# Attention in front of quantised convolutions: the products with exponentials take the transposed image, and the output projection moves behind the normalisation

## The chip, the cores and the metric

The kernel runs on one core of a Trainium2 chip. The metric is the device time of one execution in microseconds (us), lower is better. The engines are named as in the profile: PE is TensorE's matmul and PEld its weight load, DVE is VectorE, ACT is ScalarE, POOL is GpSimd, SP is SyncE.

## The reference

The input is a batch of 16 images of 128 channels and 32 x 32 pixels. Layer 0 is attention with 4 heads over the 1024 pixels of an image, and a residual; layer 1 is two 3 x 3 convolutions with 4-bit activations and weights, each followed by a batch norm over the whole batch.

```python
qkv = einsum('bchw,oc->bohw', x, w_qkv) + b_qkv          # 4 heads, 3 x 128 channels each
scores = einsum('bnc,bcm->bnm', q, k) * c ** -0.5         # 1024 x 1024 per head
attn = softmax(scores, axis=-1)
out = einsum('bnm,bmc->bnc', attn, v)                     # heads side by side: 512 channels
x = einsum('bchw,oc->bohw', out, w_out) + b_out + x       # layer 0

out = conv3x3(act_quant(x), weight_quant(w1))
out = batchnorm(out, gamma1, beta1)
out = conv3x3(act_quant(out), weight_quant(w2))
x = batchnorm(out, gamma2, beta2) + x                     # layer 1
```

`act_quant` clips to 0..1 and rounds to 15 levels, `weight_quant` rounds to 7 levels on each side.

## The kernel before

All of it stands in `fast_path`. A channel is a partition, and a pixel is a column. The weights of a head are folded at the start: query and key weights into one 128 x 128 matrix `at_sb`, value and output weights into another, `bt_sb` (`fold_a`, `fold_b`). So a head needs `u = at x` (`project_u`), scores as products of `x` with `u`, exponentials, and products of the exponentials with `vo`, which is the image already behind the value and output weights (`project_v`). The product of exponentials and `vo` is then the head's share of the output, not yet divided by the sums.

The attention phase is one loop of steps. A head `g` has `NK = 4` steps, and 63 of the 64 heads are done in this way; the last one is cut into 16 smaller units at the end. A step `k` of a head takes two blocks of 128 keys (`k` and `k + 4`) and all 1024 queries:

- `scores(g, k)`: four score tiles of 128 x 512, three PSUM banks in turn (`ps_s`), and an exponential on ScalarE for each. VectorE then makes the sums and differences T3, T1 and T2, T4 of the four blocks and adds T4 and T3 to the running sums `es`.
- `attend(g, k - 1)` for the step before: seven products of 64 x 512 in place of eight. They are a fast scheme for 2 x 2 blocks: blocks of the exponentials and their sums on one side, blocks of the values and their sums `S1` to `S4` on the other. They add up in four banks, `a0` to `a3`, over the four steps of the head.
- every f32 product is issued as two halves of 64 output rows (`halves`), which run side by side on the array.

What else a head or an image needs is hung on a step and on one of its halves with `at(step, half, fn)`: half 0 is run between `scores` and `attend`, half 1 behind `attend`. `end = (g + 1) * NK` is the first step after a head. On it hang `sum_up` (the head's sums), `evacuate` (four copies from PSUM to `ev`), `combine` in three parts (small copies of 64 partitions on ScalarE, L605 to L615, additions on VectorE, L608 to L618), and `normalise` (`end + 2`, half 1). In `normalise` the head's output is multiplied by the inverse sums and added to `accs[b]`; the last head of an image adds the bias and the image too, and stores it to `x1d`:

```python
if h == 0:
    nc.vector.tensor_tensor(accs[b], av, rb, ALU.mult)                      # L673
    return
nc.vector.tensor_tensor(av, av, rb, ALU.mult)                               # L675
nc.vector.tensor_tensor(accs[b], accs[b], av, ALU.add)                      # L676
if h == NH - 1 or g == LAST - 1:
    nc.vector.scalar_tensor_tensor(accs[b], accs[b], bo2_sb, xt[b], ALU.add, ALU.add)   # L679
```

Behind the last head of an image come `quantize`, `transform_rows`, four `rows_product` (the first convolution in a row-filtered form, bf16, PSUM tiles `psw`), `rows_output` and `first_statistics`. `project_v` of the next image makes eight tiles `psv`, spread over six steps; ScalarE copies each to `vo` (L530), VectorE makes the sums of blocks (L532, L533). `psu`, `psv` and `psw` all use the one bank of the pool `ps_m`, each freed by a copy on ScalarE.

TensorE's order is as written: each product is chained behind the one before (`issue_after`). On the other engines the framework orders the instructions by its own estimate of when their operands are there, so `quantize` and the like can stand between the operations of a step, and loads can stand earlier than where they are written.

At the end of attention the units of the last head alternate `score_unit` and `attend_unit`; `normalise_group` finishes three groups of columns, each with its row sums from a small product `psr` in the bank of `ps_m`; `first_conv` follows. The second part of the kernel does the batch norms and the second convolution and writes the output.

Of the kernel before, what the change touches and what calls it, by code (L numbers as in the profile page):

```python
# [191 lines left out]
def fast_path(  # L192
    nc, tc, x, wqk, wvo, bo, bnp, x1d, y1d, out, bo_sb, bnp_sb, quad, wq, sc, flag, conv_weights,
# [179 lines left out]
    with ExitStack() as ph:  # L373
# [4 lines left out]
        vp = pool("vo", 5)  # L378
        ep = pool("e", 2)
        esp = pool("es", 1)  # L380
        avp = pool("av", 1)
# [13 lines left out]
        xt, us, vos, es, sides, avs, psa, accs, evs = {}, {}, {}, {}, {}, {}, {}, {}, {}  # L395
# [20 lines left out]
        def load(b, queue=nc.sync):  # L416
            xt[b] = xp.tile([P, N], F32, tag="x", name=f"x{b}")
            queue.dma_start(out=xt[b], in_=x[b])

# [10 lines left out]
        nc.sync.dma_start(out=wvo_sb[0 : P // 2], in_=wvo[0 : P // 2])  # L430
        nc.scalar.dma_start(out=wvo_sb[P // 2 :], in_=wvo[P // 2 :])

        def load_rest(behind):

            with tc.issue_after(behind):
                nc.scalar.dma_start(out=wqk_sb[:, 1:], in_=wqk[:, 1:])
                nc.scalar.dma_start(out=bo_sb, in_=bo)
                nc.scalar.dma_start(out=bnp_sb, in_=bnp)
# [11 lines left out]

        bt_sb = once.tile([P, 2, NH + 1, P], F32, name="bt_sb")
        bo2_sb = once.tile([P, 1], F32, name="bo2_sb")

        def place_of(b, h):

            return h if b == B - 1 else (h + 1) % NH
# [15 lines left out]
        def fold_b():  # L474
            ps = ps_m.tile([P, NH, P], F32, tag="mm", name="ps_b")
            for h in range(NH):
                product(ps[:, h, :], wvo_sb[:, h, 0:P], wvo_sb[:, h, P : 2 * P])
            nc.scalar.copy(bt_sb[:, 1, 1:], ps)
            nc.vector.tensor_copy(bt_sb[:, 1, 0], ps[:, NH - 1])
            nc.scalar.copy(bt_sb[:, 0, :, TOP], bt_sb[:, 1, :, TOP])  # L480
            nc.vector.tensor_tensor(
                bt_sb[:, 0, 0:NH, BOTTOM], bt_sb[:, 1, 0:NH, BOTTOM], bt_sb[:, 1, 0:NH, TOP], ALU.subtract
            )
            nc.vector.tensor_copy(bt_sb[:, 0, NH, BOTTOM], bt_sb[:, 1, NH, BOTTOM])
# [30 lines left out]

        A11, A12, S3, A22, S2, S1, S4 = range(7)
# [3 lines left out]
        def project_v(b, k, c, ps=None):  # L520

            if ps is None:
                ps = ps_m.tile([P, HALF], F32, tag="mm", name=f"psv_{b}_{k}_{c}")
            first = int(b == B - 1)
            weights = bt_sb[:, c, first : first + NH].rearrange("p h o -> p (h o)")
            halves(ps, lambda t: xt[b][:, ts((k + NK * c) * 2 + t, PH)], weights)
            if c == 0:
                vos[b, k] = vp.tile([P, 7, NH, PH], F32, tag="vo", name=f"vo_{b}_{k}")
            v = vos[b, k]
            nc.scalar.copy(v[:, c : c + 3 : 2], ps.rearrange("p (h a o) -> p a h o", a=2, o=PH))  # L530
            if c == 1:
                nc.vector.tensor_tensor(v[:, S2], v[:, S3], v[:, A22], ALU.subtract)  # L532
                nc.vector.tensor_tensor(  # L533
                    v[:, S1 : S4 + 1],
                    v[:, A11 : A12 + 1],
                    v[:, S2 : S2 + 1].to_broadcast([P, 2, NH, PH]),
                    ALU.add,
                )

# [3 lines left out]
        def scores(g, k, between=None):  # L543
# [4 lines left out]
            for i, (c, m) in enumerate(((0, 1), (1, 1), (0, 0), (1, 0))):  # L548
                ps = ps_s.tile([P, HALF], F32, tag="s", name=f"pss_{g}_{k}_{i}")
                score(ps, b, g, k + NK * c, ts(m, HALF))  # L550
                exps[:] = [nc.scalar.activation(e[:, 2 * c + 1 - m], ps, AF.Exp).ins]  # L551
                if between and i in between:
                    between[i]()
# [13 lines left out]
        def attend(g, k):  # L567
            b, h = heads[g]
            e, v = es.pop((g, k)), vos[b, k][:, :, place_of(b, h)]
# [6 lines left out]
            seven = [(0, 0, A11, B11), (1, 1, A22, T4), (1, 0, A12, B21), (2, 1, S2, T2)]  # L576
            seven += [(2, 0, S4, B22), (3, 1, S1, T1)]
            if k % 2:
                seven = [seven[i] for i in (1, 0, 3, 2, 5, 4)] + [(0, 1, S3, T3)]
            else:  # L580
                seven += [(3, 0, S3, T3)]
            for n, (bank, t, value, exponential) in enumerate(seven):
                product(
                    psa[g][bank][LANES[t]],
                    v[:, value],
# [81 lines left out]
        def normalise(g):  # L667
            b, h = heads[g]
            rb = inverse_sums(g, sides.pop(g), slice(0, N))
            av = avs.pop(g)  # L670
            if h == 0:
                accs[b] = accp.tile([P, N], F32, tag="acc", name=f"acc_{b}")
                nc.vector.tensor_tensor(accs[b], av, rb, ALU.mult)  # L673
                return
            nc.vector.tensor_tensor(av, av, rb, ALU.mult)  # L675
            nc.vector.tensor_tensor(accs[b], accs[b], av, ALU.add)  # L676
            if h == NH - 1 or g == LAST - 1:

                nc.vector.scalar_tensor_tensor(accs[b], accs[b], bo2_sb, xt[b], ALU.add, ALU.add)  # L679
            if h == NH - 1:  # L680
# [26 lines left out]
        def attend_unit(u):  # L707
# [18 lines left out]
            for m, key in enumerate(keys):  # L726
                c, k = divmod(key, NK)
                v = vos[b, k][:, :, place_of(b, h)]
# [3 lines left out]
                        lambda t: v[:, (A11, S3)[t] + c],  # L732
# [129 lines left out]
        at(NK, 0, fold_bo)  # L862
# [7 lines left out]
        for g in range(LAST):  # L870
# [12 lines left out]
            if h == NH - 1:  # L883
                at(end + 3, 0, lambda b: quantize(b, accs[b], A_LEVELS, 0.0), b)
                at(end + 3, 1, sums_range, b)
                at(end + 4, 0, transform_rows, b)
                for i, k in enumerate((1, 2, 0, 3)):
                    at(end + 6 + (i + 1) // 2, (i + 1) % 2, rows_product, b, k)
                at(end + 8, 1, rows_output, b)
                at(end + 9, 0, first_statistics, b)  # L890
                if b + 2 < B:
                    at(end + 5, 0, load, b + 2, nc.scalar)
            elif h == NH - 2 and b + 1 < B:

                when = ((4, 0), (4, 1), (6, 1), (7, 0), (7, 1), (8, 0), (8, 1), (9, 1))
                for i, (step, half) in enumerate(when):
                    at(g * NK + step, half, project_v, b + 1, *divmod(i, 2))
# [4 lines left out]
        for step in range(n_steps):  # L902
            g, k = divmod(step, NK)
            between = {}
            if step == 1:
                banks = [ps_a.tile([P, HALF], F32, tag=f"a{2 + c}", name=f"psv_0_{c}") for c in range(2)]
                between = {0: lambda: project_v(0, 0, 0, banks[0]), 1: lambda: project_v(0, 0, 1, banks[1])}
            scores(g, k, between)
            if step == 0:
                fold_b()  # L910
            elif step < NK:
                project_v(0, step, 0)
# [3 lines left out]
            if 0 < step < NK:  # L916
                ps = ps_s.tile([P, HALF], F32, tag="s", name=f"psv_0_{step}_1")
                project_v(0, step, 1, ps)
# [3 lines left out]
        for u in range(n_units):  # L922
# [5 lines left out]
            if u > 3:  # L928
                for _ in range(2 if u in (8, 9) else 1):
                    attend_unit(next_)  # L930
                    next_ += 1
                    if next_ == FIRST_UNIT[1]:
                        at(n_steps + 2, 1, normalise_group, 0)
# [259 lines left out]
def attention_then_quantized_convs(  # L1193
    ctx: ExitStack,
    tc: tile.TileContext,
    x: bass.AP,
    wqk: bass.AP,
# [45 lines left out]
    def conv_weights(n, wp, behind):  # L1243
# [22 lines left out]
        nc, tc, x, wqk, wvo, bo, bnp, x1d, y1d, out, bo_sb, bnp_sb, quad, wq, sc, flag, conv_weights,  # L1266
# [83 lines left out]
```

## Time and profile before

| | |
|---|---|
| median of two runs | 2023.55 us (2023.24 to 2023.87) |
| profiled execution | 2024.57 us |
| its span | 2022.7 us |
| granted clock in it | 0.993 |
| busy: PE, PEld | 1987.6, 730.3 us |
| busy: DVE, ACT, POOL | 1722.2, 1198.5, 19.7 us |
| moved by DMA | 43.74 MB |

A line of the groups gives line and engine, the operation, what is written and read, how many there were, then busy time and the mean of one in ns, then the idle time of the engine before them and what ended it. A product of TensorE leaves two records if it is f32. A line of the timeline begins with start and length in us.

### The profile page before, as it was taken

What the parts mean: (1) busy time and instruction counts of PE and PEld (TensorE: products, weight loads), DVE (VectorE), ACT (ScalarE), POOL (GpSimd) and SP (SyncE); (2) the same over time, 40 slices, a digit from 0 to 9 for tenths busy, and PEclk for the clock granted to TensorE, in tenths of its full rate; (3) what the DMA queues carried; (4) which work ended last, traced back from release to release, by engine and by line L of the source; (5) the groups of instructions that cost most, each with busy time, mean ns of one, the idle gap of its engine ahead of it and who ended that gap; (6) DMA issues with size and microseconds to landing.
All of it is one profiled execution on the core that took longest, in us unless ns stands there. A gap on an engine that the chain in (4) does not pass through costs nothing. (4 is left out here: it accounts for less than half of the span.)

```text
span 2022.7 us, 24701 instructions
## 1 busy us (share of the span) xinstructions
PE 1987.6 (98%) x9497; PEld 730.3 (36%) x9497; DVE 1722.2 (85%) x2642; ACT 1198.5 (59%) x2007; POOL 19.7 (1%) x29
## 2 busy tenths in 40 slices
PE   9999999999999999999999999999999999999994
PEld 3543333333333333333333333433333333333441
DVE  5889888888888888888888888888888888878888
ACT  4565665665566566566556556656656655655575
POOL 0000000000000000000000000000000000000020
PEclk9999999999999999999999999999999999999997
DMA  1000000000000000000000000000000000000064
GB/s 42 24 1 22 1 22 1 22 0 1 22 1 22 1 9 14 0 22 1 21 1 1 22 1 21 11 22 11 1 22 11 22 11 21 11 1 11 11 239 168
DMA packets 12846, 43.74 MB, mean 22 GB/s; under 512 B 1456, under 2 KB 1840, under 8 KB 12720
## 3 DMA queue, kind: packets, MB, share of 16 engines
q1 hardware_dynamic: 9520, 32.05, 4.2%
q10 hardware_dynamic: 3200, 10.03, 1.5%
q8 instruction: 76, 1.25, 0.3%
q14 instruction: 50, 0.41, 0.1%
HBM read 22.16 MB, written 19.92 MB: 21 GB/s over the span
## 5 line engine op out<-in xcount | busy, mean ns | idle before, releaser
L403 PE MATMUL pss<-u,x 128*64 128x512 f32 (+1 forms) x4128 | 1031.9, 589 | 1.6 <-ACT u L509 1.6
L403 PE MATMUL psa<-e,vo 128*64 128x512 f32 (+1 forms) x3624 | 922.4, 588 | 0.0
L551 ACT ACTIVATE e<-pss 128x512 f32<-128x512 f32 x1008 | 595.4, 596 | 380.7 <-PE pss L403 331.9
L403 PEld LDWEIGHTS pss<-u,x 128*64 128x64 f32 x4128 | 351.6, 137 | 549.3 <-issue 493.4
L403 PEld LDWEIGHTS psa<-e,vo 128*64 128x64 f32 x3624 | 304.8, 137 | 483.5 <-issue 449.6
L555 DVE TENSOR_TENSOR e<-e 128x1024 f32<-128x1024 f32 x252 | 307.7, 1221 | 29.8 <-ACT e L551 21.6
L554 DVE TENSOR_TENSOR e<-e 128x512 f32<-128x512 f32 x252 | 172.2, 683 | 105.5 <-ACT e L551 101.7
L558 DVE TENSOR_TENSOR e<-e 128x512 f32<-128x512 f32 x252 | 174.0, 690 | 21.5 <-DVE e L555 0.5
L595 ACT COPY ev<-psa 128x512 f32<-128x512 f32 x252 | 135.5, 589 | 87.2 <-PE psa L403 87.0
L403 PE MATMUL psu<-x,at_sb 128*64 128x512 f32 x512 | 184.9, 599 | 1.0 <-DMA x<-in_x_dram 1.0
L403 PE MATMUL psv<-bt_sb,x 128*64 128x512 f32 x512 | 184.9, 592 | 1.0 <-ACT bt_sb L480 1.0
L530 ACT COPY vo<-psv 128x512 f32<-128x512 f32 x128 | 75.5, 590 | 142.3 <-PE psv L403 142.3
L564 DVE TENSOR_TENSOR es<-es,e 128x1024 f32<-128x1024 f32 x126 | 154.0, 1222 | 2.7
L509 ACT ACTIVATE u<-psu,au_sb 128x512 f32<-128x512 f32 x127 | 87.4, 688 | 21.7 <-PE psu L403 20.1
L798 ACT ACTIVATE m<-psw 128x512 f32<-128x512 f32 x60 | 35.9, 598 | 92.6 <-PE psw L403 90.7
L608 DVE TENSOR_TENSOR y<-ev,y 128x512 f32<-128x512 f32 x63 | 43.6, 692 | 52.4 <-ACT y L606 52.4
L664 DVE STREAM_TRANSPOSE rb<-sums 128x1024 f32<-128x1024 f32 (+1 forms) x66 | 79.8, 1210 | 1.6
L625 DVE TRANSPOSE_TENSOR_REDUCE part<-es 128x32 f32<-128x1024 f32 (+1 forms) x65 | 79.6, 1224 | 1.1
L403 PEld LDWEIGHTS psv<-bt_sb,x 128*64 128x64 f32 x512 | 53.6, 137 | 73.5 <-issue 66.7
L403 PEld LDWEIGHTS psu<-x,at_sb 128*64 128x64 f32 x512 | 53.5, 138 | 73.1 <-issue 69.1
L562 DVE TENSOR_TENSOR es<-e,e 128x1024 f32<-128x1024 f32 x63 | 76.8, 1219 | 0.0
L675 DVE TENSOR_TENSOR av<-av,rb 128x1024 f32<-128x1024 f32 x47 | 57.6, 1225 | 1.6
(159 smaller groups left out, 1193.6 us busy)
## 6 DMA issues: line engine op xcount, KB each, us to landing
x_dram<-acc SPq DMA_DIRECT2D x16, 512.0 KB, 4.3
x<-in_x_dram ACTq DMA_DIRECT2D x15, 512.0 KB, 4.6
res<-x_dram SPq DMA_DIRECT2D x1, 7680.0 KB, 30.0
y_dram<-y SPq DMA_DIRECT2D x6, 512.0 KB, 2.6
back<-y_dram SPq DMA_DIRECT2D x1, 3072.0 KB, 11.4
out_dram<-back SPq DMA_DIRECT2D x6, 512.0 KB, 4.5
out_dram<-y SPq DMA_DIRECT2D x5, 512.0 KB, 4.1
out_dram<-y SPq DMA_DIRECT2D x9, 256.0 KB, 2.5
```

The source lines that it names most:

```text
L403: done = nc.tensor.matmul(out_, lhsT=lhsT, rhs=rhs, start=start, stop=stop)
L509: copied = nc.scalar.activation(dst, ps, AF.Identity, bias=au_sb[:, h : h + 1])
L530: nc.scalar.copy(v[:, c : c + 3 : 2], ps.rearrange("p (h a o) -> p a h o", a=2, o=PH))
L551: exps[:] = [nc.scalar.activation(e[:, 2 * c + 1 - m], ps, AF.Exp).ins]
L554: nc.vector.tensor_tensor(e[:, T3], e[:, B12], e[:, B22], ALU.add)
L555: nc.vector.tensor_tensor(e[:, T1 : T2 + 1 : T2 - T1], e[:, B12 : B11 + 1], e[:, B11 : T3 + 1 : T3 - B11], ALU.subtract)
L558: nc.vector.tensor_tensor(e[:, T4], e[:, T2], e[:, B21], ALU.add)
L562: nc.vector.tensor_tensor(sides[g], es[g, 0][:, T4 : T3 + 1], mine, ALU.add)
L564: added = nc.vector.tensor_tensor(sides[g], sides[g], mine, ALU.add)
L595: nc.scalar.copy(to, ps)
L625: nc.vector.tensor_reduce(part, total.rearrange("p (k c) -> p k c", c=Q), AX.X, ALU.add, apply_transpose=True,)
L664: nc.vector.transpose(rb, rinv.unsqueeze(2).to_broadcast([P, n, Q]))
```

## The change

The values and the output projection are taken apart again. `xT`, the image with pixels as partitions, is laid out on the host as one more input, and the products with the exponentials take it directly in place of `vo`; since it is the same for all heads, the block sums are made once per image (`sum_values`). What comes out of a head is then the image averaged with that head's attention. It is normalised as before, kept for all four heads (`avs`, five buffers in place of one), and `project_out` multiplies it with `bt_sb` and adds up the four heads in PSUM, one half of the columns at a time, in the bank of `ps_m`. VectorE takes the sum out of PSUM together with bias and residual. The last head of all takes values made by `last_values`, so it needs no projection behind it. The steps behind an image move back by one or two, `fold_b` moves from step 0 to step 5, and `wvo` is loaded later. The small copies on VectorE (`side`, `sums`) stay as they are.

```diff
-        vp = pool("vo", 5)
+        vp = pool("xt", 2)
+        lastp = pool("vlast", 1)
-        avp = pool("av", 1)
+        avp = pool("av", 5)
...
         def load(b, queue=nc.sync):
             xt[b] = xp.tile([P, N], F32, tag="x", name=f"x{b}")
             queue.dma_start(out=xt[b], in_=x[b])
+            load_transposed(b, queue)
+        S3, S2, S1, S4 = range(4)
+        def load_transposed(b, queue):
+            t = vp.tile([P, NCH, P], F32, tag="xt", name=f"xt_{b}")
+            vs[b] = (t, vp.tile([P, 4, NK, PH], F32, tag="xs", name=f"xs_{b}"))
+            queue.dma_start(out=t, in_=xT[b])
+        def sum_values(b):
+            t, s = vs[b]
+            nc.vector.tensor_tensor(s[:, S3], t[:, 0:NK, BOTTOM], t[:, 0:NK, TOP], ALU.subtract)
+            nc.vector.tensor_tensor(s[:, S2], s[:, S3], t[:, NK:, BOTTOM], ALU.subtract)
+            nc.vector.tensor_tensor(
+                s[:, S1 : S4 + 1],
+                t[:, :, TOP].rearrange("p (a k) c -> p a k c", a=2),
+                s[:, S2 : S2 + 1].to_broadcast([P, 2, NK, PH]),
+                ALU.add,
+            )
...
-        nc.sync.dma_start(out=wvo_sb[0 : P // 2], in_=wvo[0 : P // 2])
-        nc.scalar.dma_start(out=wvo_sb[P // 2 :], in_=wvo[P // 2 :])
+        load_transposed(0, nc.sync)
         def load_rest(behind):
             with tc.issue_after(behind):
                 nc.scalar.dma_start(out=wqk_sb[:, 1:], in_=wqk[:, 1:])
+                nc.scalar.dma_start(out=wvo_sb, in_=wvo)
...
         def fold_b():
-            ps = ps_m.tile([P, NH, P], F32, tag="mm", name="ps_b")
+            ps = ps_s.tile([P, NH, P], F32, tag="s", name="ps_b")
             for h in range(NH):
                 product(ps[:, h, :], wvo_sb[:, h, 0:P], wvo_sb[:, h, P : 2 * P])
-            nc.scalar.copy(bt_sb[:, 1, 1:], ps)
...
+            nc.scalar.copy(bt_sb, ps)
...
-        def project_v(b, k, c, ps=None):
...
+        def last_values(i):
+            b, h = heads[LAST]
+            if i == 0:
+                vs["last"] = lastp.tile([P, NCH, P], F32, name="vlast")
+            ps = ps_m.tile([P, NK, P], F32, tag="mm", name=f"psv_{i}")
+            for n in range(NK):
+                halves(
+                    ps[:, n], lambda t: xt[b][:, ts(2 * (i * NK + n) + t, PH)], bt_sb[:, h, :]
+                )
+            nc.scalar.copy(vs["last"][:, ts(i, NK)], ps)
...
-            e, v = es.pop((g, k)), vos[b, k][:, :, place_of(b, h)]
+            e, (t, s) = es.pop((g, k)), vs[b]
+            A11, A12 = t[:, k, TOP], t[:, NK + k, TOP]
+            A22 = t[:, NK + k, BOTTOM]
...
         def normalise(g):
-            b, h = heads[g]
             rb = inverse_sums(g, sides.pop(g), slice(0, N))
-            av = avs.pop(g)
-            if h == 0:
+            nc.vector.tensor_tensor(avs[g], avs[g], rb, ALU.mult)
+        def project_out(b, hf):
+            if hf == 0:
                 accs[b] = accp.tile([P, N], F32, tag="acc", name=f"acc_{b}")
-                nc.vector.tensor_tensor(accs[b], av, rb, ALU.mult)
-                return
-            nc.vector.tensor_tensor(av, av, rb, ALU.mult)
-            nc.vector.tensor_tensor(accs[b], accs[b], av, ALU.add)
-            if h == NH - 1 or g == LAST - 1:
-                nc.vector.scalar_tensor_tensor(accs[b], accs[b], bo2_sb, xt[b], ALU.add, ALU.add)
-            if h == NH - 1:
+            mine = [g for g in range(b * NH, (b + 1) * NH) if g != LAST]
+            ps = ps_m.tile([P, HALF], F32, tag="mm", name=f"pso_{b}_{hf}")
+            for g in mine:
+                halves(
+                    ps,
+                    lambda t: bt_sb[:, heads[g][1], LANES[t]],
+                    avs[g][:, ts(hf, HALF)],
+                    start=(g == mine[0]),
+                    stop=(g == mine[-1]),
+                )
+            some = ts(hf, HALF)
+            nc.vector.scalar_tensor_tensor(
+                accs[b][:, some], ps, bo2_sb, xt[b][:, some], ALU.add, ALU.add
+            )
+            if hf == NHF - 1 and b < B - 1:
                 nc.sync.dma_start(out=x1d[b], in_=accs[b])
...
-        at(NK, 0, fold_bo)
+        at(NK + 1, 1, fold_b)
+        at(NK + 2, 0, fold_bo)
...
             if h == NH - 1:
-                at(end + 3, 0, lambda b: quantize(b, accs[b], A_LEVELS, 0.0), b)
-                at(end + 3, 1, sums_range, b)
-                at(end + 4, 0, transform_rows, b)
+                for hf in range(NHF):
+                    at(end + 4, hf, project_out, b, hf)
+                at(end + 5, 0, sums_range, b)
+                at(end + 5, 1, lambda b: quantize(b, accs[b], A_LEVELS, 0.0), b)
+                if b + 2 < B:
+                    at(end + 5, 1, load, b + 2, nc.scalar)
+                at(end + 6, 0, transform_rows, b)
                 for i, k in enumerate((1, 2, 0, 3)):
-                    at(end + 6 + (i + 1) // 2, (i + 1) % 2, rows_product, b, k)
-                at(end + 8, 1, rows_output, b)
-                at(end + 9, 0, first_statistics, b)
-                if b + 2 < B:
-                    at(end + 5, 0, load, b + 2, nc.scalar)
+                    at(end + 7 + i // 2, i % 2, rows_product, b, k)
+                at(end + 9, 1, rows_output, b)
+                at(end + 10, 0, first_statistics, b)
             elif h == NH - 2 and b + 1 < B:
-                when = ((4, 0), (4, 1), (6, 1), (7, 0), (7, 1), (8, 0), (8, 1), (9, 1))
-                for i, (step, half) in enumerate(when):
-                    at(g * NK + step, half, project_v, b + 1, *divmod(i, 2))
+                at(end + 1, 1, sum_values, b + 1)
+        for i in range(2):
+            at(n_steps - 4, i, last_values, i)
+            at(n_steps + 3, i, project_out, B - 1, i)
...
                     if next_ == FIRST_UNIT[1]:
-                        at(n_steps + 2, 1, normalise_group, 0)
+                        at(n_steps + 3, 0, normalise_group, 0)
```

## The prediction

> **What bounds the kernel now.** I read the views in this order: the busy table of the page, the table by stage for three stretches of two images each, the groups by form, the timeline of TensorE at the start, the timeline of all engines around one end of a head, and the timeline of the tail.
>
> ```profile
> PE 1987.6 (98%) x9497; PEld 730.3 (36%) x9497; DVE 1722.2 (85%) x2642; ACT 1198.5 (59%) x2007; POOL 19.7 (1%) x29
> ...
> L403 PE MATMUL psu<-x,at_sb 128*64 128x512 f32 x512 | 184.9, 599 | 1.0 <-DMA x<-in_x_dram 1.0
> L403 PE MATMUL psv<-bt_sb,x 128*64 128x512 f32 x512 | 184.9, 592 | 1.0 <-ACT bt_sb L480 1.0
> L530 ACT COPY vo<-psv 128x512 f32<-128x512 f32 x128 | 75.5, 590 | 142.3 <-PE psv L403 142.3
> ```
>
> A busy TensorE (PE) is not yet a full one, so I compare it with its own pace. The first product with `rows` comes once per image at the same place of the program:
>
> ```profile
> 426.42 1.03 PE L403 MATMUL psw<-rows,middle 128*64 128x512 bf16 x5
> ...
> 665.17 1.03 PE L403 MATMUL psw<-rows,middle 128*64 128x512 bf16 x5
> ...
> 903.92 1.03 PE L403 MATMUL psw<-rows,middle 128*64 128x512 bf16 x5
> ...
> 426.42:665.17 238.75, 238.75 (x1139) 84.04 (x1137) 204.92 (x307) 142.45 (x242) 0.00 (x0) 1.00 0.03 10
> 665.17:903.92 238.75, 238.75 (x1139) 84.05 (x1137) 205.08 (x307) 142.45 (x242) 0.00 (x0) 1.00 0.03 10
> ```
>
> (The columns of the last two: length, then busy time of PE, PEld, DVE, ACT and POOL, clock, DMA.) Two images take 238.75 us every time, 119.38 us for one. The program gives one image 272 f32 products of 64 rows (128 of scores, 112 of attention, 16 of `psu`, 16 of `psv`) and 24 of bf16. An f32 product leaves two records, and in a run of scores 16 records take 3.43 us (1002.27 to 1005.70), 0.214 us each. 544 x 0.214 = 116.6, and 24 bf16 products, 0.65 us for each six, are 2.6: 119.2 us. TensorE waits for nothing in the steady part. VectorE (DVE) is busy 102.5 of the 119.4 us, ScalarE (ACT) 71.2.
>
> The start and the tail have small waits:
>
> ```profile
> 10.05 3.65 PE L403 MATMUL pss<-u,x 128*64 128x512 f32 x16 [0.79 <-ACT u L509]
> 13.63 1.16 PE L403 MATMUL ps_b<-wvo_sb 128*128 128x128 f32 x8
> 14.72 1.08 PE L403 MATMUL pss<-u,x 128*64 128x512 f32 x4
> 16.84 1.08 PE L403 MATMUL psv<-bt_sb,x 128*64 128x512 f32 x4 [1.04 <-ACT bt_sb L480]
> ```
>
> And one tight place, at each end of a head (1008.9 is the end of the last product of the head before):
>
> ```profile
> 1015.18 0.62 ACT L612 COPY ev<-y 64x512 f32<-64x512 f32 x1
> ...
> 1016.43 1.22 DVE L562 TENSOR_TENSOR es<-e,e 128x1024 f32<-128x1024 f32 x1
> ...
> 1017.75 1.20 ACT L551 ACTIVATE e<-pss 128x512 f32<-128x512 f32 x2 [0.58 <-DVE es L562]
> ```
>
> The third group of exponentials may overwrite a buffer only after VectorE has added the first two (`es`). It starts at 1017.75, frees its score bank at 1018.35, and the fourth score product wants that bank at 1018.58: 0.23 us of slack.
>
> **What the Trainium skill says.** "TensorE: Matmul & The Clock Gate", in "Wait — 56ns, not 53.3ns?", gives 215.7 ns from start to start for 512 columns on a warm array. Here two halves side by side start two records every 0.43 us, which agrees: nothing but fewer products makes this part shorter. The same page, "Architectural detail", says that ScalarE and VectorE are strictly first in, first out; every `es` wait above is such a queue. "VectorE: DVE Perf Modes", "Why PSUM operands drop a tier", leaves f32 from PSUM at the plain rate; L1039, an f32 operation of two tensors on 512 elements from PSUM, took 668 ns against 690 from SBUF, so I price the new eviction at 0.67.
>
> **The change part by part.**
>
> *TensorE.* Gone: 256 products `psv` of 512 columns. New: 16 images x 2 halves x 4 heads x 2 = 256 of `pso`, less 4 (the last head is not projected), and 16 of 128 columns for the last head's values, worth 4. The sum is zero: 110 us go and 110 us come. Scores, attention and `psu` keep number and shape.
>
> *VectorE.* Gone: L532 26.9, L533 44.1, L676 57.4, L679 20.5 = 148.9 us. New: sums over the transposed image, 32 x 0.42 and 16 x 0.69 = 24.4; evictions 32 x 0.67 = 21.4. Net 103 us less, 1619. *ScalarE:* L530 goes, 75.5 us; about 1124 stays. Neither is on the path in the steady part, so I credit 0.
>
> *DMA.* 16 more loads of 512 KB, 8.39 MB, at 1 to 3% DMA share. The built order puts the transposed load on ScalarE's queue just behind L612 and the sums that read it behind VectorE's normalising multiply of the same head. L612 stands 6.3 us after the end of the head before, so the issue is near 6.9; the `x` loads landed in 4.6 us: 11.5. VectorE gets there at 11.1 (its multiply ended at 1020.1). It waits 0.4 us, spends 1.4 on the sums, and the next T4, at 13.9 now, comes near 16; TensorE wants it at 18 (four scores 3.4, `psu` 0.9, attention 3.0, twice, and scores again). Hidden, with 2 us to spare. At the start the transposed image takes the place of `wvo` (514 KB landed at 8.3); its sums are done long before 16.9, where attention begins. `wvo` itself is loaded later and folded in step 5, in line.
>
> *Start.* Scores of step 0 end at 13.5. With no fold and no `psv` between, those of step 1 end at 16.9 and attention follows. Before, it began at 21.6, with 2.6 us of `psv` and 0.9 of `ps_b` in between: 21.6 - 16.9 - 3.5 = 1.2 us of waiting goes. **-1.2.**
>
> *End of an image.* `pso` of half 0, attention of the head before (3.0), `pso` of half 1 and then `psu` share one PSUM bank, which VectorE now empties. The order has the first eviction behind T4 of the new head; VectorE, after the sums of the head before, reaches it 1.5 us before half 1 wants the bank. The second stands behind L613. From the end of attention: the four `ev` copies end at 1.5 (as in the trace), three half copies follow, L608 runs at 2.8, L612 at 3.5, L613 at 4.2, the eviction at 4.8 to 5.5; `psu` wants the bank at 6.9. No wait on the bank. But the order puts L615 and the first exponential ahead of the 1.06 us Relu: first exponential 5.5, Relu 6.1 to 7.1, second 7.7. On VectorE follow L617, L618, the multiply (to 7.8), T3, quantising, T1/T2, quantising, T4, a row transform and `es`: 0.6 for each of 512, 1.15 for each of 1024, `es` ends at 13.0 and frees the exponentials of the next step. They release the score bank at 13.65; TensorE, 3.44 us later for `pso`, wants it at 13.4. So the slack of 0.23 turns into a stall of 0.2 to 0.3. One head later the row outputs (1.15 and two statistics of 0.6) come before `es` while TensorE gets only 0.65 us for `psw`: 0 to 0.2. I take 0.3 for an image; bounds 0 (durations a little kinder) and 1.0 (each step of the chain 0.07 longer). 15 x 0.3 = **+4.5**, 0 to 15.
>
> *Values of the last head.* Each group of `psv` follows `psw` at once in the same bank: the first waits for a 0.6 copy (0.9 with its latency), the second for the four `ev` copies and one more (2.15 - 0.65 = 1.5). **+2.4.**
>
> *Tail.* Counted from the end of the last score product S. Before, S is 1924.7 and the last quantised row is ready at 1931.4, S + 6.7. After, `psv` of the last image (6.9 less 1.7 for the small ones, so 5.15) and the first `psr` (0.4) are not yet behind it, so S comes 5.55 earlier, and `pso` must follow. `pso` half 0 ends at S + 2.6; `psr` waits in the same bank for its eviction, 3.5; half 1 ends at 7.3; VectorE normalises and quantises group 0 (4.2 to 8.0) before the second eviction, 8.8; `psr` of group 1 to 9.4, last attention to 11.1, last `psr` 11.6, and VectorE's chain of group 1 and 2, 12 operations of 0.25 to 0.45, ends at S + 14.7. 14.7 - 6.7 - 5.55 = **+2.4**, with 0 to 4 as bounds. Convolutions and output behind it are as before.
>
> Sum: -1.2 + 4.5 + 2.4 + 2.4 = +8.1. The profiled execution took 2024.57 us, its span 2022.7 and 1.87 around it; I expect 2032.7 of its like, and against the median of 2023.55 **2031.6**.
>
> **The rivals.**
> - *All absorbed.* The image ends keep their slack and the tail hides under the longer TensorE work: only -1.2 and +2.4, 2024.8. For it: VectorE has 103 us less to do. Against: the order puts the new work exactly into the tight stretch.
> - *The transposed image lands late.* VectorE stands in its queue at the sums. Beyond the 2 us to spare, each us costs 15; with 4 us more than worked out, 2 x 15 = 30, so 2061. For: the issue is only 4 us ahead of the use. Against: 4.9 was the slowest landing of an `x` load.
> - *The bank that VectorE empties becomes the bound*, the case on the other side. Place: `pso` half 0 to half 1 and on to `psu`. If VectorE's backlog at the end of an image holds the eviction 1.5 us longer nothing happens; from 4.2 us on, 2.7 us of stall x 15 = 40.5 us are 2%. At 5.5 us, 4 x 15 = 60 + 3.6: 2087. For: one bank, and an in-order queue at 85%. Against: the load falls, and T4 sits ahead of the eviction in any case.
> - *VectorE was the hidden bound*: its 103 us come off, 1920. Against: the steady image equals TensorE's pace to 0.2 us.
>
> **How the numbers follow.** Forecast (2025 to 2042) 0.60; absorbed 0.22; late image or other stalls of 2 to 3 us, 0.09; the bank 0.07; VectorE 0.02. Over 2% (40 us) is about what a measurement of this kernel can tell from no change: faster 0.02, same 0.91, slower 0.07. The range takes in the absorbed case and the bounds of the image ends and the tail: 2021 to 2052.
>
> **What would show it.** Right: the distance of the first `psw` of two images is 238.8 to 239.6; `pso` has about 504 records; VectorE near 1620 busy and ScalarE near 1125; the third group of exponentials in the image-end head waits for `es`; attention starts near 17 us; `psr` waits for the eviction of `pso`. Wrong: two images over 241 us apart, a PE wait named after the eviction of `pso` or after the load, or a tail from S to the last row well off 14.7.

## The result, and the profile after

The change makes the kernel slower by one per cent: 2043.86 us (2043.22 to 2044.49) against 2023.55, ratio 1.01 with a 95% interval of 1.0057 to 1.0144. Run again beside the kernel before on one chip it was 2043.39 against 2024.28, ratio 1.0097 (1.0082 to 1.0113). The forecast was 2031.6: the direction and most of the steps are right, and the size is 12 us short. The spans of the two profiled executions, 2042.6 and 2022.7, differ by 19.9 us, and this sum is accounted for below.

The busy line of the page after:

```profile
PE 2003.8 (98%) x9521; PEld 1113.3 (55%) x9521; DVE 1633.9 (80%) x2528; ACT 1121.1 (55%) x1880; POOL 19.7 (1%) x29
```

Two groups by form of the kernel after, the weight loads of the output products and the evictions (busy time, mean of one in ns, idle before):

```profile
L404 PEld LDWEIGHTS pso<-av,bt_sb 128*64 128x64 f32 x504 | 62.4, 137 | 45.6 <-issue 40.4
...
L686 DVE SCALAR_TENSOR_TENSOR acc<-pso,bo_sb,x 128x512 f32<-128x512 f32 x32 | 23.9, 745 | 0.5 <-PE pso L404 0.5
```

VectorE lost 88 us and ScalarE 77 us of work, as the change intends, and nothing of it arrived. No weight load of an output product waited for an eviction: the only idle time named before them is "issue", time in which the engine waited for nothing that the profile shows. The evictions waited 0.5 us in all for their products. This speaks against the single PSUM bank, and VectorE's emptying of it, as the cause. PE still reads 98%, and that figure hides the loss. The distance of the first `psw` of two images shows it, in the timeline:

```profile
665.03 0.61 PE L404 MATMUL psw<-rows,middle 128*64 128x512 bf16 x2
...
905.87 0.61 PE L404 MATMUL psw<-rows,middle 128*64 128x512 bf16 x2
```

And in the table by stage of the same kernel (length, then busy times of PE, PEld, DVE, ACT, POOL):

```profile
665.03:905.87 240.84, 240.84 (x1140) 136.26 (x1137) 193.96 (x293) 132.65 (x226) 0.00 (x0) 1.00 0.04 14
```

Two images take 240.84 us where they took 238.75: 1.04 us per image, 15.6 us for 15 images. That is nearly all of the 19.9. Laid against a steady pace (0.2145 us for each f32 record, starts averaged over eight records), TensorE's products fall behind at four places in an image, by 0.30, 0.35, 0.25 and 0.16 us. Together that is 1.06 us, the whole of the loss within the error of the reading. (The recorded expectations put the four at 0.29, 0.21, 0.17 and 0.21, together 0.88.) Each time it is the same product: the fourth score of a step, which reuses the PSUM bank of the first. The first two places are in the head in which the output products run, which is the second head of the next image; the recorded texts call it the head that ends an image. This is the timeline of ScalarE, VectorE and the weight loads there; the weight load of a waiting product is what carries the wait:

```profile
1129.90 0.61 ACT L615 COPY ev<-y 64x512 f32<-64x512 f32 x1 [0.76 <-DVE y L613]
...
1130.54 0.60 ACT L551 ACTIVATE e<-pss 128x512 f32<-128x512 f32 x1
...
1131.16 1.06 ACT L255 ACTIVATE qt<-acc 128x1024 f32<-128x1024 f32 x1
1131.19 0.20 PEld L404 LDWEIGHTS pss<-u,x 128*64 128x64 f32 x4 [0.69 <-ACT e L551]
...
1136.80 1.22 DVE L560 TENSOR_TENSOR es<-e,e 128x1024 f32<-128x1024 f32 x1
...
1138.11 1.65 ACT L551 ACTIVATE e<-pss 128x512 f32<-128x512 f32 x3 [3.85 <-DVE es L560]
...
1138.76 0.35 PEld L404 LDWEIGHTS pss<-u,x 128*64 128x64 f32 x4 [0.51 <-ACT e L551]
```

In step 1 the five half copies (L605 to L615) all stand before the first exponential. The last of them has itself waited 0.76 us for VectorE's L613, and the exponential follows it at once and ends at 1131.14; the fourth product's weights are let in at 1131.19. The quantisation's Relu (L255) stands behind that exponential, so it is not what made it late. In step 2 the exponentials wait for `es`, and the fourth product for the first of them. The other two places are one head later, and the first of them has a ScalarE operation in front that the prediction did not look at, the eviction of the fourth row product (L805):

```profile
1159.98 0.61 ACT L805 ACTIVATE m<-psw 128x512 f32<-128x512 f32 x1
...
1161.14 0.59 ACT L551 ACTIVATE e<-pss 128x512 f32<-128x512 f32 x1
...
1161.78 0.19 PEld L404 LDWEIGHTS pss<-u,x 128*64 128x64 f32 x3 [0.45 <-ACT e L551]
...
1168.53 1.09 ACT L551 ACTIVATE e<-pss 128x512 f32<-128x512 f32 x2 [1.78 <-DVE es L560]
...
1169.18 0.19 PEld L404 LDWEIGHTS pss<-u,x 128*64 128x64 f32 x3 [0.35 <-ACT e L551]
```

In the waits of the whole run the two rows that answer to this grew: the wait for `es` was 46.9 us in 46 cases before, and that of a score's weight load for an exponential 17.8 in 67. After:

```profile
ACT e L551 <- DVE es L560: 103.1, 60, 3.9
...
PEld pss L404 <- ACT e L551: 39.0, 94, 0.7
```

Start and tail, from the timeline:

```profile
17.26 1.03 PE L404 MATMUL psa<-e,xt 128*64 128x512 f32 x4
...
1935.23 1.03 PE L404 MATMUL pss<-u,x 128*64 128x256 f32 x8
...
1939.69 0.40 PE L404 MATMUL psr<-part,quad 128*128 128x16 f32 x2 [0.85 <-DVE acc L686]
...
1944.88 0.61 PE L404 MATMUL psr<-part,quad 128*128 128x8 f32 x4 [1.20 <-DVE acc L686]
...
1950.33 0.30 DVE L257 TENSOR_SCALAR pad<-qt 128x256 bf16<-128x256 f32 x1
```

And the transposed load, in the DMA issues of the page (KB each, us to landing):

```profile
xt<-in_xT_dram ACTq DMA_DIRECT2D x15, 512.0 KB, 3.5
```

Attention starts at 17.26. The last score ends, and the next product starts, at 1936.1, 11.4 us later than before, and the last quantised row is there at 1950.63, 14.5 us behind it. VectorE waited for the transposed image once, 0.6 us.

### The profile page after: what moved, and what is told of

Read it like the earlier page. It is cut to its first block, busy times and chain, and to the rows that moved or that the text cites. A ratio compares the mean times of both kernels' runs of the same rounds, so it can differ in the third digit from the quotient of the medians.

```text
span 2042.6 us, 24529 instructions
## 1 busy us (share of the span) xinstructions
PE 2003.8 (98%) x9521; PEld 1113.3 (55%) x9521; DVE 1633.9 (80%) x2528; ACT 1121.1 (55%) x1880; POOL 19.7 (1%) x29
## 5 line engine op out<-in xcount | busy, mean ns | idle before, releaser
L404 PE MATMUL pss<-u,x 128*64 128x512 f32 (+1 forms) x4128 | 1046.6, 590 | 1.6 <-ACT u L519 1.6
L404 PEld LDWEIGHTS pss<-u,x 128*64 128x64 f32 x4128 | 488.8, 137 | 405.5 <-issue 281.2
L404 PE MATMUL psa<-e,xs 128*64 128x512 f32 x2016 | 632.4, 592 | 0.0
L404 PE MATMUL psa<-e,xt 128*64 128x512 f32 x1512 | 506.1, 592 | 0.0
L404 PEld LDWEIGHTS psa<-e,xs 128*64 128x64 f32 x2016 | 259.5, 137 | 167.5 <-issue 115.8
L553 DVE TENSOR_TENSOR e<-e 128x1024 f32<-128x1024 f32 x252 | 308.1, 1223 | 21.0 <-ACT e L551 11.4
L404 PEld LDWEIGHTS psa<-e,xt 128*64 128x64 f32 x1512 | 192.6, 137 | 158.0 <-issue 134.0
L404 PE MATMUL psu<-x,at_sb 128*64 128x512 f32 x512 | 169.5, 600 | 1.2 <-issue 1.2
L404 PE MATMUL pso<-av,bt_sb 128*64 128x512 f32 x504 | 126.2, 592 | 0.0
L404 PEld LDWEIGHTS pso<-av,bt_sb 128*64 128x64 f32 x504 | 62.4, 137 | 45.6 <-issue 40.4
L669 DVE TENSOR_TENSOR av<-av,rb 128x1024 f32<-128x1024 f32 x63 | 77.1, 1224 | 2.0
```

The lines of the kernel that those rows point to most:

```text
L404: done = nc.tensor.matmul(out_, lhsT=lhsT, rhs=rhs, start=start, stop=stop)
L553: nc.vector.tensor_tensor(e[:, T1 : T2 + 1 : T2 - T1], e[:, B12 : B11 + 1], e[:, B11 : T3 + 1 : T3 - B11], ALU.subtract)
L669: nc.vector.tensor_tensor(avs[g], avs[g], rb, ALU.mult)
```

## The experiments

The queue theory, as it stood before the runs: what the change lost stands in the order of the in-order queues of ScalarE and VectorE. An image's quantisation, and a head later the evicted row products and the output rows, come ahead of the first exponential of step 1 or of `es`, and the fourth score product waits for its bank. (For the first of the four places the trace above already names another operation, the half copy L615.) Rival 1: the output products' one bank and its eviction. Rival 2: TensorE itself has more to do per image. "Period" below is the distance of the first `psw` of two images (238.75 before, 240.84 after), from the table by stage of each run.

**The later places, in the kernel before**

```diff
-                at(end + 3, 0, lambda b: quantize(b, accs[b], A_LEVELS, 0.0), b)
-                at(end + 3, 1, sums_range, b)
-                at(end + 4, 0, transform_rows, b)
+                at(end + 5, 0, sums_range, b)
+                at(end + 5, 1, lambda b: quantize(b, accs[b], A_LEVELS, 0.0), b)
+                at(end + 6, 0, transform_rows, b)
...
-                    at(end + 6 + (i + 1) // 2, (i + 1) % 2, rows_product, b, k)
-                at(end + 8, 1, rows_output, b)
-                at(end + 9, 0, first_statistics, b)
+                    at(end + 7 + i // 2, i % 2, rows_product, b, k)
+                at(end + 9, 1, rows_output, b)
+                at(end + 10, 0, first_statistics, b)
```

> The kernel before, with the rows, their products and the output rows of an image put at the steps that the changed kernel gives them (one to one and a half steps later); nothing else is taken from the change: no products with the transposed image, no output products in PSUM. Queue theory (what the change lost per image is the place of the quantised image and of the output rows ahead of a head's first partial sum in the queues of VectorE and ScalarE): only the second place is imitated here, the output rows at a head's step 1, which the changed kernel pays with 0.17 + 0.21 = 0.38 us per image; 15 images make 5.7 us, so about 2029 us. Rival 1 (the output products' single PSUM bank and its eviction cost the time) and rival 2 (TensorE itself has more to do per image): neither is in this kernel, so 2023.5 us, within 1.5 us of the kernel before.

Measured: 2031.33 us, ratio 1.0031 (1.0019 to 1.0042), period 239.39. The kernel before becomes slower without any of the new products: 0.32 us per image, 4.8 us, where 5.7 was expected. This is the largest part of the 6.3 us that the ratio gives; the rest was not located.

**Quantisation behind the step's exponentials and `es`**

```diff
-                at(end + 5, 1, lambda b: quantize(b, accs[b], A_LEVELS, 0.0), b)
+                at(end + 5, 1, behind, lambda b: quantize(b, accs[b], A_LEVELS, 0.0), b)
...
+        def behind(fn, *args):
+            with tc.issue_after(exps[0]), tc.issue_after(sums_added[0]):
+                fn(*args)
```

(`sums_added` is now set at step 1 too.)

> The changed kernel, with the quantisation of an image kept behind the step's exponentials on ScalarE and behind the first partial sum on VectorE; nothing else moves. Queue theory: the two delays of the fourth score product in the head that ends an image (0.29 + 0.21 us) go, 0.5 x 15 = 7.5 us, so about 2036 us, and two images 239.8 us apart instead of 240.8. Rival 1 (bank and eviction of the output products): they are as they were, so 2043.9 us within 1.5, two images 240.8 apart. Rival 2 (TensorE has more to do): the same, 2043.9 us.

Measured: 2034.53 us, ratio 1.0054 (1.004 to 1.0068), period 239.67. One ScalarE and two VectorE instructions per image changed places, and 0.585 us per image came back, 8.8 us. The bank, its evictions and TensorE's work are as they were, so rivals 1 and 2 fall as main causes. The size fits, but the places are not those that were expected:

```profile
1003.76 0.62 ACT L616 COPY ev<-y 64x512 f32<-64x512 f32 x1 [0.76 <-DVE y L614]
...
1004.40 0.60 ACT L551 ACTIVATE e<-pss 128x512 f32<-128x512 f32 x1
...
1005.05 0.20 PEld L404 LDWEIGHTS pss<-u,x 128*64 128x64 f32 x4 [0.69 <-ACT e L551]
```

The wait in step 1 still stands, behind the same half copy (L616 in this run), and TensorE still falls behind by some 0.25 us there. So the quantisation is not its cause. What went is the wait in step 2, behind `es`, and one of the two waits a head later, where this run changes nothing; why that one went was not found out. No run moves the half copy alone, so its part in step 1 is read from the trace and not shown by an experiment.

**Output rows behind the first partial sum, a head later**

```diff
-                at(end + 9, 1, rows_output, b)
+                at(end + 9, 1, behind, rows_output, b)
```

> The changed kernel, with the output rows of an image, one head later, kept behind that step's exponentials and first partial sum; the quantisation stays where the change put it. Queue theory: the two delays of the fourth score product in that head (0.17 + 0.21 us) go, 0.38 x 15 = 5.7 us, so about 2038 us, two images 240.1 us apart. Rivals 1 and 2: 2043.9 us within 1.5, two images 240.8 apart.

Measured: 2041.49 us, ratio 1.0087 (1.0073 to 1.0101), period 240.58. Only 0.13 of 0.38 us came back: a miss. The output rows account for a part of the wait behind `es` (the fourth score's weight load of step 2 waits 0.22 us instead of 0.35); the late first exponential of step 1 is not theirs. ScalarE's timeline in this run shows the eviction of the fourth row product still in front of that exponential, which led to the next run:

```profile
797.28 0.62 ACT L806 ACTIVATE m<-psw 128x512 f32<-128x512 f32 x1
...
798.44 0.59 ACT L551 ACTIVATE e<-pss 128x512 f32<-128x512 f32 x1
```

**The same, with the row products half a step earlier**

```diff
-                    at(end + 7 + i // 2, i % 2, rows_product, b, k)
+                    at(end + 6 + (i + 1) // 2, (i + 1) % 2, rows_product, b, k)
```

> The kernel with the output rows kept behind the first partial sum, and in addition the four products of the rows half a step earlier, where the kernel before has them. The run with the output rows alone took away only 0.13 of the 0.38 us in that head; the rest (0.17 + 0.13 us) still stands. Queue theory, on ScalarE: it is the eviction of the fourth of these products (0.62 us) that stands in front of the first exponential of step 1; half a step earlier it is out of the way, so 0.30 x 15 = 4.5 us go against that run, two images 240.58 - 0.60 = 239.98 us apart, about 2037 us on that run's scale. Rival: the delay comes with the output product's heads themselves (the combining copies of that head, or the PSUM bank shared by products): then the period stays at 240.6 and the time at about 2041.5 us.

Measured: 2036.64 us, ratio 1.0066 (1.0053 to 1.008), period 240.20. In this run no fourth score of that head is late any more. The gain is 0.19 us per image instead of the expected 0.30, since the two delays one head earlier grew: they now make all of the 0.72 us per image that the period still lies above 238.75. The gain of the period makes 2.9 us of the 4.9 between the two runs. At the last head's values, weight loads waited 2.7 us behind `psw` in two waits before and 1.2 us in one here; the rest was not located.

**Everything at an image's end later**

```diff
-                    at(end + 4, hf, project_out, b, hf)
-                at(end + 5, 0, sums_range, b)
-                at(end + 5, 1, lambda b: quantize(b, accs[b], A_LEVELS, 0.0), b)
+                    at(end + 5 + hf, 1, project_out, b, hf)
+                at(end + 7, 0, sums_range, b)
+                at(end + 7, 0, lambda b: quantize(b, accs[b], A_LEVELS, 0.0), b)
...
-                at(end + 9, 1, rows_output, b)
-                at(end + 10, 0, first_statistics, b)
+                at(end + 12, 0, rows_output, b)
+                at(end + 12, 0, first_statistics, b)
```

(The load moves to `end + 7`, the rows to `end + 7` half 1, their products to steps `end + 9` to `end + 11`.)

> The changed kernel, with everything at an image's end put later in the order written out by hand: output products at the second half of steps 1 and 2 of that head, quantisation at its step 3, rows, their products and the output rows up to two steps later, so that none of it stands ahead of a head's first partial sum. The products and evictions are the same in number, and still share one PSUM bank. Queue theory: all four delays go, 0.88 x 15 = 13 us, two images 238.8 to 239.2 us apart, about 2030 us; if the shifted work finds another narrow place, some of it comes back. Rival 1 (bank and eviction): 2043.9 us or more, since TensorE meets the bank at later points but just as often. Rival 2 (TensorE has more to do per image): 2043.9 us within 2.

Measured: 2027.07 us, ratio 1.0014 (1.0008 to 1.0021). The table by stage of this kernel:

```profile
677.69:916.77 239.08, 239.08 (x1140) 131.04 (x1137) 193.89 (x293) 132.32 (x226) 0.00 (x0) 1.00 0.04 14
```

From 240.84 to 239.08 is 0.88 us per image, 13.2 us, the sum that was expected. In the trace all four delays are gone, which is more than that, and a new one has come: what is left, 0.16 us per image, is again a fourth score, behind the 1.06 us Relu at step 3. The values no longer wait for `psw` either.

**One step earlier instead**

```diff
-                    at(end + 4, hf, project_out, b, hf)
+                    at(end + 3, hf, project_out, b, hf)
...
-                at(end + 5, 1, lambda b: quantize(b, accs[b], A_LEVELS, 0.0), b)
+                at(end + 4, 0, lambda b: quantize(b, accs[b], A_LEVELS, 0.0), b)
```

(Rows, their products and the output rows move forward with them, and the last image's output products have the bank of the next experiment.)

> The changed kernel with the output products, the quantisation, the rows and their products one to one and a half steps earlier, which is where the kernel before has quantisation and rows; the last image's output products go to a PSUM bank of their own. Queue theory: nothing stands ahead of a first partial sum any more, two images 238.8 to 239.3 us apart; the output rows' half of the loss goes too; with the tail's wait of 2.05 us for the eviction gone, about 2026 us. Against it: the output products stand nearer to the normalisation that feeds them, so TensorE may have to wait for VectorE there; if it waits 0.5 us per image, 7.5 us come back (2033). Rival (bank and eviction, or TensorE's own work): 2042 us.

Measured: 2027.95 us, ratio 1.0018 (1.0009 to 1.0026), period 239.20. Both directions out of the tight place work. No product waited for the normalisation; one fourth score still lags by 0.17 us.

**Later, Relu behind the exponentials, own bank in the tail**

```diff
-                at(end + 7, 0, lambda b: quantize(b, accs[b], A_LEVELS, 0.0), b)
+                at(end + 7, 0, behind, lambda b: quantize(b, accs[b], A_LEVELS, 0.0), b)
...
-            ps = ps_m.tile([P, HALF], F32, tag="mm", name=f"pso_{b}_{hf}")
+            bank, tag = (ps_a, "a3") if b == B - 1 else (ps_m, "mm")
+            ps = bank.tile([P, HALF], F32, tag=tag, name=f"pso_{b}_{hf}")
```

(`behind` holds only for the exponentials here.)

> The version with everything at an image's end later (two images 239.08 us apart), and two things more: the quantisation's Relu behind the step's exponentials on ScalarE, which takes the last delay (0.10 us at a fourth score product behind that 1.06 us Relu), and a PSUM bank of its own for the last image's output products. Queue theory: 0.10 to 0.16 us per image less, 1.5 to 2.4 us, two images 238.75 to 238.9 us apart; the tail's wait of 0.85 + 1.20 us at the sums' products goes, so that the last quantised row comes 12.5 us after the last score instead of 14.5. Together 3.5 to 4.5 us under the 2027.1 us of that version: about 2023 us, level with the kernel before (2024.4 in that set). If the sums' products in the tail wait for the output products themselves and not for the bank, the 2 us stay: 2025 us.

Measured: 2023.25 us, ratio 0.9994 (0.9986 to 1.0003). Table by stage and tail of this kernel:

```profile
676.15:914.91 238.76, 238.76 (x1139) 86.38 (x1137) 193.64 (x293) 133.22 (x226) 0.00 (x0) 1.00 0.04 14
```

```profile
1915.66 1.03 PE L404 MATMUL pss<-u,x 128*64 128x256 f32 x8
...
1929.47 0.30 DVE L257 TENSOR_SCALAR pad<-qt 128x256 bf16<-128x256 f32 x1
```

The period is that of the kernel before, and so is the time. All parts of the change are in it, with the same 504 records of `pso`. So the whole loss in the steady part came from where the work stood and not from the work itself, and taking 90 us from VectorE gains nothing. The tail got shorter by 1.3 us instead of 2: `psr` no longer waits for the eviction, and the last row comes 13.25 us behind the last score. It is level with the kernel before, not faster.

**Doses: what one late exponential costs**

An extra, unused copy on ScalarE between the evacuating copies and the first exponential of step 1, in the version just shown. By its condition (`h == 0`) it stands in the first head of an image, one head ahead of the output products, where this version has no other work of an image's end. So it tests the hand-over of the bank in step 1 by itself:

```diff
+            if k == 1 and h == 0 and b > 0:
+                with tc.issue_after(copied4[0]):
+                    first = nc.scalar.copy(dose, xt[b][:, 0:n]).ins
```

> The version with everything later and its own bank, with one more ScalarE copy per image, 128x8, put between the four evacuating copies and the first exponential of step 1 in the head that ends an image; its result is not used. In that version the first exponential ends 0.38 us before the fourth score product wants its bank, and two images are 238.75 us apart. A copy this small should take 0.2 us (worked out from the exponent of 512 columns at 0.60 and the two-column-size copies; an estimate). Proportional theory (a delay beyond the slack is passed on one to one) and step theory (a late bank costs a fixed restart of about 0.2 us, whatever the lateness): both expect nothing here, 238.75. Rival to the queue theory (ScalarE's place in the queue does not matter): 238.75 for all three doses.

> As the small dose, with a copy of 128x256 (estimate 0.4 us). Proportional theory: slack of 0.38 less the time of the signal, so 0.05 to 0.15 us late, two images 239.0 +- 0.1 us apart. Step theory: about 0.2 us per image, two images 239.15. Rival: 238.75.

> As the small dose, with a copy of 128x512 (0.60 us). Proportional theory: 0.25 to 0.35 us late, two images 239.3 to 239.45 us apart. Step theory: still about 0.2 us, 239.15. Rival: 238.75. If further fourth products of the same head get late too, more than either.

> As the full dose, with two such copies (2 x 0.63 = 1.26 us per image). The single full dose cost 0.165 us per image and half of it nothing, so the slack there is between 0.42 and 0.63 us; if lateness is passed on one to one it is 0.63 - 0.165 = 0.47. Proportional theory: 1.26 - 0.47 = 0.79 us late per image, less 0.1 if the copies that follow the first exponential are moved by the new order, so 0.7 to 0.8, two images 240.15 to 240.35 us apart. Step theory (a late bank costs a fixed 0.17 to 0.2 us per product): 0.17 to 0.4, two images 239.1 to 239.5.

The total times of these single runs scatter by some us through the start of the kernel, so the period is read. Without a dose, with one of 512 columns, and with two (first copy of the evacuation, dose, first exponential, the fourth product's weight load), one fence for each kernel:

```profile
725.79 1.07 ACT L595 COPY ev<-psa 128x512 f32<-128x512 f32 x2 [1.12 <-PE psa L404]
...
728.02 0.62 ACT L551 ACTIVATE e<-pss 128x512 f32<-128x512 f32 x1
```

```profile
729.31 2.28 ACT L606 COPY ev<-psa 128x512 f32<-128x512 f32 x4 [1.12 <-PE psa L404]
731.47 0.63 ACT L554 COPY dose<-x 128x512 f32<-128x512 f32 x1
731.99 0.61 ACT L560 ACTIVATE e<-pss 128x512 f32<-128x512 f32 x1
...
732.65 0.37 PEld L404 LDWEIGHTS pss<-u,x 128*64 128x64 f32 x4 [0.49 <-ACT e L560]
```

```profile
734.82 2.05 ACT L608 COPY ev<-psa 128x512 f32<-128x512 f32 x4 [1.12 <-PE psa L404]
736.74 0.65 ACT L554 COPY dose<-x 128x512 f32<-128x512 f32 x1
737.41 0.62 ACT L618 COPY y<-ev 64x512 f32<-64x512 f32 x1
738.05 0.62 ACT L556 COPY dose<-x 128x512 f32<-128x512 f32 x1
738.57 0.59 ACT L562 ACTIVATE e<-pss 128x512 f32<-128x512 f32 x1
...
739.22 0.20 PEld L404 LDWEIGHTS pss<-u,x 128*64 128x64 f32 x4 [1.78 <-ACT e L562]
```

| dose | one copy, us | first exponential after the first evacuating copy | period | lost per image |
|---|---|---|---|---|
| none | | 2.23 | 238.76 | 0 |
| 8 columns | 0.21 | 2.33 | 238.75 | 0 |
| 256 | 0.42 | 2.52 | 238.75 | 0 |
| 512 | 0.63 | 2.68 | 239.09 | 0.17 |
| 512 twice | 2 x 0.65 | 3.75 | 241.19 | 1.22 |

The dose stands behind the fourth evacuating copy, and the exponential starts before the dose has ended: 0.10, 0.31 and 0.52 us behind the start of a single dose of 0.21, 0.42 and 0.63 us. So the exponential moves by less than the copy takes. Up to 2.52 nothing is lost. Between the last two rows the exponential is 1.07 us later and 1.05 us more is lost: lateness is passed on one to one, and the step theory falls. The two rows also give the same slack: 0.45 us later less 0.17 lost is 0.28, 1.52 less 1.22 is 0.30. The forecast for the double dose (0.7 to 0.8) was too small mainly because a half copy slid in between the two doses and added its own 0.6 us; that for the half dose (0.05 to 0.15) was too large because the exponential moved by only 0.29 us.

**The change once more**

> The changed kernel once more, beside the kernel before on the same chip, so that the sum of the terms can be held against a narrower interval. From the two profiles the change costs 2042.6 - 2022.7 = 19.9 us, ratio 1.0098; both theories expect 1.009 to 1.011.

Measured: ratio 1.0097 (1.0082 to 1.0113), as expected.

## Why the prediction was right or wrong

- *TensorE neutral, VectorE and ScalarE worth nothing:* right. The version with later places and its own bank has all of the new products and the old period, 238.76. The forecast of the busy times was 1619 and 1124; 1634 and 1121 came. Added up one by one, VectorE's instructions became 102.6 us shorter, as worked out; its busy time counts records that overlap once and fell by 88.
- *Transposed load hidden:* right; the wait was 0.6 us in all, so the rival of the late image falls. So does the one in which VectorE was the hidden bound: the change takes 88 us from it and is slower.
- *The bank as the bound:* rightly set low. No output product waited for an eviction in the steady part; only the small `psr` products in the tail did.
- *Start and last values, -1.2 and +2.4:* about right together. The last score is 11.4 us later; with 15.6 us for the images and 5.55 us of work moved behind it, 1.35 us remain for both, where 1.2 was forecast. They can't be told apart well: first scores began between 9.34 and 10.34 us in runs whose start is the same, which is as much as the start's term.
- *Tail, S + 14.7:* right, 14.5; the two waits for the eviction (0.85 and 1.20) are there. 14.5 - 6.75 - 5.55 = 2.2 us.
- *End of an image, 0.3 us:* this is the term that was mis-sized. It measured 1.04 us per image, 15.6 us instead of 4.5, just over its own upper bound of 15. The places in the hand-made schedule were good: first exponential at 5.5 us (1130.54, with the zero at 1125.0), `es` to 13.0 (1138.02), bank free at 13.65 (1138.71). What failed is what was compared. The working tested one hand-over of a bank, that of the exponential behind `es`. It did not put the same question to step 1, although it had the numbers: a first exponential from 5.5 to 6.1, and a fourth score that wants the bank 12 records of 0.214 us behind `pso`, at 3.44 + 2.57 = 6.0. A head later it looked at VectorE alone, while the eviction of the fourth row product stood in front on ScalarE. So it counted one stall, with a share for a second, where there were four, of 0.16 to 0.35 us.
- *Its own signs:* the wait for `es`, the 504 records of `pso`, the start of attention and the wait of `psr` came as named. The distance of two images did not: 240.84 us lies above the 238.8 to 239.6 named as right and just below the 241 named as wrong. The total lies inside the forecast's range because that range was wide; the term that carries the change left its own bounds.

The sum by the runs: 15.6 + 1.35 + 2.2 = 19.2 us, and 0.7 us between the last quantised row and the end of the span make 19.9.

## What to carry to other kernels

In a loop where the bound engine hands PSUM banks round, list every product that reuses a bank and ask for each when its releaser starts. In the doses here, all the time by which an operation put in front on ScalarE moved the releasing exponential beyond the slack was lost, although ScalarE was busy for only 56% of the span. Test the first exponential of a step as well as the one behind the obvious wait, and both queues. If work must be added at a tight place, move it by a step first: here the places were worth some 17 of the 20 us (ratio 1.0097 to 1.0014), and the exchange of work itself nothing in the steady part.

## What the runs showed of the hardware

- A waiting score's weight load started 0.64 to 0.66 us after the start of the exponential that frees its bank (0.59 to 0.61 us long where it stands alone), so some 0.05 us behind its end, at each of the six places shown above, whether the wait was 0.35 or 1.78 us.
- On ScalarE the exponential behind a dose started before that copy had ended, 0.52 us behind the start of one of 0.63 us, so a copy in front delayed it by less than its length. A half copy behind a dose did not: 0.67 us behind the start of one of 0.65.
- The eviction that takes its sum out of PSUM and adds bias and residual takes 745 ns for 128x512, where 668 for one tensor fewer had been the nearest row.
- Busy PEld, which counts loads that overlap once, is no measure of loads: 767 us in the last version (later places, own bank), 1113 us in the changed kernel, for 9521 loads each. Busy PE is none of stalls: it fills all 240.84 us of the slower two images.
